# Weighing expert rows on ScalarE, moving layer 0's openings, and routing both choices at once in a two-layer kernel

## The chip, the cores and the metric

The kernel runs on one core of one Trainium2 chip. The metric is the device time of one execution in microseconds (us). The engines are named as in the profile: PE is TensorE (matmul), PEld its weight loads, DVE is VectorE, ACT is ScalarE, POOL is GpSimd, and SP is SyncE, which here only issues DMAs.

## What is computed

Two layers work on x of 2 x 2048 tokens by 256 channels. Each layer computes `x + s(xn) * silu(g(xn))`, where xn is the layer norm of x, s is one branch and g the other.

```
layer 0:  s = linear attention (16 heads of 16, rotary, elu + 1), times W_out
          g = block: h = ln(xn);  x' = xn + softmax attention(h) W_proj     (causal, per batch; 2048 tokens, 16 heads of 16)
              flat = ln(x');  gates = softmax(flat Wgate);  top 2 of 8 experts, 1024 slots for each expert
              exp_in[e, pos] = flat[token];  exp_out = gelu(exp_in W1 + b1) W2 + b2
              g = x' + sum over the 2 choices of gate * exp_out[e, pos]     (gate 0 where no slot is left)
layer 1:  s = softmax attention (causal; 16 heads, queries, keys and values of 32) Wo
          g = x int4(kernel) + bias + (x a) b
```

## The kernel before

Everything is float32 apart from small masks. Tokens stand in 32 tiles of 128 rows (`xr`, 16 tiles for each batch). The kernel has three stages: layer 0's attention with routing and linear attention; the experts; layer 1 with its attention and gate. Four heads share the 128 partitions, 32 rows for each, so that four score matmuls run side by side in row groups. A **head group** is four heads of one batch, and there are eight in each layer.

`run_attention` (L515) writes the attention of both layers in **units**. For a head group, pass A computes scores for the row maxima (tile t of queries against 512 keys, L536), which DVE reduces (L543 on the diagonal, L547 elsewhere). Pass B, started later, computes the transposed scores (L562), of which ACT takes the exponential (L574) into one of the tiles `pt`. A unit holds four matmuls of pass A and four pairs of pass B, and takes all 8 PSUM banks. Per group there are 40 units of pass A and 36 of pass B. After every second block of keys, and at the end of a block of 256 queries, follow the **sums** (L804 in layer 0; L1508 and L1514 in layer 1): column-tiled matmuls of `pt` with the values. In layer 1 POOL first adds up the exponentials (L1490 to L1495) for the denominators.

All other work is emitted as steps of **strands**: `prep` (norms and projections of the next head group, full-array matmuls), `lin` (linear attention, `lin_keys` and `lin_out`), `moe` (`route`), `send`, `end` (`finish`, `residual`), `mix`, `gate`. Every step names its engine, an expected cost, and what it reads and writes. The class `Plan` then orders all steps: a greedy beam search over the steps' costs, with a handicap for each strand, picks for each engine the next step that can start first. The resulting order of each engine is fixed in the program. Buffers (`Buf`) are taken from small sets of slots (8 banks `s`, and in layer 1 six `pt`, one `gx` and one `xs`), and a step that needs one waits until a slot is free.

PE work of strands other than `S` (full-array work) is let in only at an **opening**: before a unit whose first step has `open = True`, and up to 2.5 us of it (`LIMIT`); if nothing else can start for 0.3 us, it goes in anyway. Before the change, a unit is open if the unit before it was followed by sums or had no pass B:

```
            if first and (u == 0 or closed):
                first.open = True
            closed = late or not b
```

`route` (L898) works on four token tiles (two at the very end): it normalises them, computes the logits, and then DVE does some sixty small instructions on 128 x 32 or 128 x 4 elements: softmax and both choices (`choose`, L943), and after a matmul that counts tokens (`count`) the slots (`places`, L964). `places` loops over the two choices; for each it computes the slot for sending (`to`), the slot for fetching (`back`) and the weight (`m`). Then POOL issues one indirect DMA for each tile and choice (`send`, L991) into `slots_in`. The first load of the experts (L1284) waits for all sends.

The experts (L1274 to L1309) run as eight times two blocks of 512 rows, without a planner.

In layer 1, `mix` (L1343) finishes layer 0 for two token tiles: SP loads `xs` (the input and the linear attention's output), POOL issues four indirect gathers into `gx` (L1357), DVE weighs the rows of both choices and adds x' (L1366, L1367, L1370), ACT applies silu (L1373), and POOL multiplies by s and adds the input (L1374, L1375). After every second `mix` the moments (L477, DVE) and roots (L482 to L485, POOL) for the norm follow. The mixes of batch 0 come ahead of the first head group, those of batch 1 at units 24, 32, ... 80.

Of the kernel before, what the change touches and what calls it, by code (L numbers as in the profile page):

```python
# [317 lines left out]
def kernel(ctx: ExitStack, tc: tile.TileContext, i: dict, out: bass.AP):  # L318
# [34 lines left out]
    def turn_pair(pair, tp=None):  # L353
# [161 lines left out]
    def run_attention(plan, make, prepare, subtract, sum_keys, finish, last_sum, before=None, others=()):  # L515
# [65 lines left out]
        sums, parts_left, pair = {}, [], []  # L581
        for u in range(at + last_sum + 1):
# [60 lines left out]
    with ExitStack() as sc:  # L643
# [226 lines left out]
        SH = [P, 4, E]  # L870

        def small(name):
            return w.tile(SH, F32, name=name)

        def line(name):
            return w.tile([P, 4], F32, name=name)
# [4 lines left out]
        def expert_row(c, of):  # L881
            return cst[:, None, c : c + E].to_broadcast([P, of, E])
# [7 lines left out]
        def first_of_largest(m, hot, src, first):  # L890

            nc.vector.tensor_reduce(m, src, AX.X, ALU.max)
            nc.vector.tensor_tensor(hot, src, wide(m), ALU.is_equal)
            nc.vector.tensor_tensor(hot, hot, expert_row(C_EREV, src.shape[1]), ALU.mult)
            nc.vector.tensor_reduce(first, hot, AX.X, ALU.max)
            nc.vector.tensor_tensor(hot, hot, wide(first), ALU.is_equal)

        def route(G, t0, of):  # L898
            n0 = G.b * NT + t0
            gates, rest, mask, before_, took, *hots = (x[:, :of] for x in smalls)  # L900
            top, tot, first, place, e_of, room, a_ = (x[:, :of] for x in lines)
            ms = [m[:, n0 : n0 + of] for _, _, m in routes]
# [40 lines left out]
            def choose():  # L943
                nc.vector.tensor_reduce(tot, gates, AX.X, ALU.add)
                nc.vector.reciprocal(tot, tot)
                nc.vector.tensor_tensor(gates, gates, wide(tot), ALU.mult)
                first_of_largest(ms[0], hots[0], gates, first)
                nc.vector.scalar_tensor_tensor(rest, hots[0], -4.0, gates, ALU.mult, ALU.add)
                first_of_largest(ms[1], hots[1], rest, first)
                nc.vector.tensor_tensor(mask, hots[0], hots[1], ALU.add)  # L950
                nc.vector.tensor_copy(before_[:, 0:1], so_far)
                for n in range(1, of):
                    nc.vector.tensor_tensor(before_[:, n : n + 1], before_[:, n - 1 : n], mask[:, n - 1 : n], ALU.add)
                nc.vector.tensor_tensor(so_far, before_[:, of - 1 :], mask[:, of - 1 :], ALU.add)
# [5 lines left out]
            def count():  # L960
                for n, (ones_, m) in enumerate(((cst[:, C_TRI : C_TRI + P], mask), (ones, before_))):
                    nc.tensor.matmul(cum.t[:, : of * E], ones_, m.rearrange("p t e -> p (t e)"), start=n == 0, stop=n == 1)
# [21 lines left out]
            S("moe", "DVE", 3.2, choose, r=["gates"], w=["hots", "mask"])  # L984
            S("moe", "PE", 0.25, count, r=["mask"], w=[cum])
            S("moe", "DVE", 3.6, places, r=[cum, "hots"], w=[("routes", n0), "gates"])
            for t in range(of):
                for to, _, _ in routes:

                    def send(to=to, t=t):  # L990
                        inst = nc.gpsimd.indirect_dma_start(  # L991
                            out=slots_in, out_offset=bass.IndirectOffsetOnAxis(ap=to[:, n0 + t : n0 + t + 1], axis=0),
# [181 lines left out]
        for b in range(B):  # L1174
# [3 lines left out]
            start, every = ((4, 7.5), (180, 7.5))[b]  # L1178
# [8 lines left out]
        run_attention(plan, Group0, prepare, subtract, sum_keys, finish, SUM_LAG0, others=others)  # L1187
# [132 lines left out]
    with ExitStack() as sc:  # L1320
# [7 lines left out]
                mx=slots(wk, "mx", 2, [P, 2, 4, 4]), pt=slots(wk, "pt", 6, [P, 4, 512]), ps=slots(wk, "ps", 2, [P, 4, QC]),  # L1328
# [5 lines left out]
                gl=slots(wk, "gl", 2, [P, 2, D]), gs=slots(wk, "gs", 2, [P, 2, D]), gx=slots(wk, "gx", 1, [P, 2, 2, D]), xs=slots(wk, "xs", 1, [P, 2, 2, D]),  # L1334
# [8 lines left out]
        def mix(n0):  # L1343
# [20 lines left out]
            def weigh():  # L1364
                for t in range(2):
                    nc.vector.tensor_scalar_mul(gx.t[:, 0, t], gx.t[:, 0, t], routes[0][2][:, n0 + t : n0 + t + 1])  # L1366
                    nc.vector.scalar_tensor_tensor(  # L1367
                        gx.t[:, 0, t], gx.t[:, 1, t], routes[1][2][:, n0 + t : n0 + t + 1], gx.t[:, 0, t], ALU.mult, ALU.add
                    )
# [285 lines left out]
```

## Time and profile before

| | |
|---|---|
| median of three runs | 3568.2 us (3566.0 to 3568.63) |
| profiled execution | 3565.2 us, span 3563.4 us |
| granted PE clock, mean | 0.964 |
| layer 0's first sums to the last | 60.9 to 1453.0 us |
| head groups of layer 0, end to end of their sums | 165.0, 170.8, 194.2, 166.1, 159.6, 162.0, 178.2 us |
| experts | first transpose at 1507.5 us, last matmul to 1976.7 us |
| first matmul of layer 1 | 2012.4 us |
| head groups of layer 1, end to end of their sums | 208.1, 170.5, 194.7, 183.9, 168.1, 168.0, 149.5 us |

In the profile's slices a digit is the busy share of a fortieth of the span, 89.1 us, in tenths. Times of one place are in us from the start of the span. A group is all instructions of one line, engine and tile; "idle before" is the time its engine stood still just ahead of it, with what ended that. A head group's end is read from the last of its 576 matmul records of the sums' line.

### The profile page before, as it was taken

How to read it: one execution, taken by the hardware profiler on the slowest of the kernel's cores; microseconds unless marked ns; L12 is line 12 of the kernel's file. 1: busy time of each engine (PE TensorE's matmuls, PEld its weight loads, DVE VectorE, ACT ScalarE, POOL GpSimd, SP SyncE). 2: the span in 40 equal slices, each digit the busy share in tenths (PEclk: the TensorE clock that was granted, in tenths of full speed). 3: DMA queues.
4: the chain of work that ended last, by engine and by line, in shares of the span. 5: the costliest groups of instructions: out<-in, count | busy, mean ns of one | idle time of the engine just before them, and what ended most of it. 6: DMA issues, size and time to landing. Idle time of an engine off the chain costs nothing.

```text
span 3563.4 us, 81449 instructions
## 1 busy us (share of the span) xinstructions
PE 3381.1 (95%) x33814; PEld 2412.0 (68%) x33814; DVE 2193.3 (62%) x5726; ACT 1667.0 (47%) x3281; POOL 1679.8 (47%) x2238
## 2 busy tenths in 40 slices
PE   6999999999999999599999599989999999999998
PEld 4767777777777777366666356656777667777775
DVE  4767676777677768511111266777677557676774
ACT  3565555555555555221111154544455554544554
POOL 3452232333332221400000466887787567878777
PEclk7999999999999999799999789998999999999999
DMA  5000000000000000212220221111000010000000
GB/s 178 2 2 2 11 8 8 16 28 14 13 8 5 19 14 12 99 61 81 66 86 24 75 66 35 34 38 34 21 14 21 31 39 19 18 14 18 16 26 22
DMA packets 88020, 115.41 MB, mean 32 GB/s; under 512 B 9043, under 2 KB 67103, under 8 KB 87650
## 3 DMA queue, kind: packets, MB, share of 16 engines
q1 hardware_dynamic: 81506, 96.32, 8.3%
q0 software_dynamic: 6144, 13.88, 1.2%
q8 instruction: 266, 4.36, 0.5%
q14 instruction: 104, 0.85, 0.1%
HBM read 75.33 MB, written 37.75 MB: 32 GB/s over the span
## 4 chain that ended last, share of the span: by engine, by line
PE 84%; POOL 5%; DVE 5%; issue 3%; ACT 2%; DMA 1%; POOLq 0%; SPq 0%; DVEq 0%; ACTq 0%
PE s L562 16%; PE s L536 16%; PE s L804 7%; PE s L1297 6%; PE s L1303 6%; PE s L1508 6%; PE s L1420 3%; PE s L736 3%; PE s L506 3%; PE s L1478 2%; PE s L1514 2%; PE s L1556 2%; PE s L359 2%; PE s L1435 2%; PE s L1057 1%
## 5 line engine op out<-in xcount | busy, mean ns | idle before, releaser
L574 ACT ACTIVATE pt<-s 128x512 f32<-128x512 f32 (+1 forms) x2304 | 1170.2, 577 | 625.5 <-PE s L1478 192.2
L562 PE MATMUL s<-qt,kt 32*128 32x256 f32 (+1 forms) x9216 | 1329.0, 390 | 9.3 <-ACT pt L574 2.5
L536 PE MATMUL s<-kt,qt 32*128 32x512 f32 (+3 forms) x5120 | 1306.2, 563 | 21.1 <-DVE mx L547 11.4
L547 DVE TENSOR_REDUCE mx<-s 128x1 f32<-128x512 f32 x1536 | 958.6, 684 | 205.8 <-PE s L536 114.5
L562 PEld LDWEIGHTS s<-qt,kt 32*128 32x128 f32 x9216 | 1023.9, 186 | 66.9 <-ACT pt L574 13.2
L536 PEld LDWEIGHTS s<-kt,qt 32*128 32x128 f32 x5120 | 560.6, 187 | 170.0 <-issue 89.8
L543 DVE CUSTOM_DVE_ANT_0 s<-s,cst 128x128 f32<-128x128 f32 (+3 forms) x1024 | 480.8, 516 | 101.7 <-PE s L536 79.5
L1490 POOL TENSOR_TENSOR ps<-pt 128x1024 f32<-128x1024 f32 (+1 forms) x160 | 347.6, 2173 | 125.5 <-ACT pt L574 104.0
L743 POOL TENSOR_TENSOR ra<-raw,rope 128x128 f32<-128x128 f32 x128 | 59.3, 463 | 676.3 <-ACT raw L755 622.0
L1494 POOL TENSOR_TENSOR ps<-ps,pt 128x1024 f32<-128x1024 f32 x128 | 302.8, 2365 | 84.5 <-ACT pt L574 78.9
L1478 PE MATMUL s<-mh,ones_h 3*128 3x512 bf16 (+1 forms) x1152 | 316.9, 370 | 0.0
L1357 POOL DMA_INDIRECT gx<-slots_out,back x64 | 62.7, 980 | 499.0 <-issue 496.7
L1306 DVE TENSOR_TENSOR ye<-s,b 128x256 f32<-128x256 f32 x64 | 27.2, 425 | 410.7 <-PE s L1303 410.7
L804 PE MATMUL s<-pt,vt 128*32 128x256 f32 (+1 forms) x4608 | 272.6, 375 | 1.6 <-ACT pt L574 1.6
L1495 POOL TENSOR_TENSOR ps<-ps,pt 128x1024 f32<-128x1024 f32 (+1 forms) x128 | 268.1, 2095 | 10.0
L1508 PE MATMUL s<-pt,vt 128*32 128x256 f32 (+1 forms) x4608 | 271.7, 374 | 0.2 <-ACT pt L574 0.2
L1298 ACT ACTIVATE hm<-s,b1c 128x512 f32<-128x512 f32 x128 | 87.9, 687 | 361.1 <-PE s L1297 361.1
L1297 PE MATMUL s<-xt,w 128*128 128x512 f32 x512 | 226.1, 600 | 7.1 <-DVE xt L1269 7.0
L1508 PEld LDWEIGHTS s<-pt,vt 128*32 128x32 f32 x4608 | 134.5, 110 | 138.9 <-issue 20.7
L1303 PE MATMUL s<-w,hm 128*128 128x256 f32 x1024 | 223.6, 379 | 0.0
L804 PEld LDWEIGHTS s<-pt,vt 128*32 128x32 f32 x4608 | 134.5, 110 | 123.7 <-issue 25.0
L1303 PEld LDWEIGHTS s<-w,hm 128*128 128x128 f32 x1024 | 194.6, 190 | 33.3 <-issue 7.7
(256 smaller groups left out, 4289.7 us busy)
## 6 DMA issues: line engine op xcount, KB each, us to landing
w<-in_L_ffn_W_dram SPq DMA_DIRECT2D x16, 1024.0 KB, 5.6
gl<-g_dram SPq DMA_DIRECT2D x64, 256.0 KB, 2.6
slots_in<-zero SPq DMA_DIRECT2D x8, 1024.0 KB, 10.1
xe<-slots_in SPq DMA_DIRECT2D x16, 512.0 KB, 5.7
slots_out<-ye SPq DMA_DIRECT2D x16, 512.0 KB, 5.2
xr<-in_L_attn_x_dram SPq DMA_DIRECT2D x4, 1024.0 KB, 8.2
s_dram<-lo SPq DMA_DIRECT2D x16, 256.0 KB, 2.0
hn<-in_L_attn_x_dram SPq DMA_DIRECT2D x16, 256.0 KB, 2.7
```

What stands on the lines that cost most here:

```text
L536: nc.tensor.matmul(s.t[:, :w], g.qt.t[r, t * P : (t + 1) * P], g.kt.t[r, 512 * k : 512 * k + w], start=True, stop=True)
L543: nc.vector.tensor_tensor_reduce(s.t[:, :w], s.t[:, :w], causal[:, 512 - w :], 1.0, -3e38, ALU.add, ALU.max, to)
L547: nc.vector.tensor_reduce(to, s.t[:, :w], AX.X, ALU.max)
L562: nc.tensor.matmul(s.t[:, at], g.kt.t[r, kj * P : (kj + 1) * P], g.qt.t[r, QC * c + q0 : QC * (c + 1)], start=n == 0, stop=n == 1 and not ...
L574: S("B", "ACT", t_act(w), lambda: nc.scalar.activation(pt.t[:, j, :w], s.t[:, :w], AF.Exp, scale=0.25), r=[s], w=[(pt, j)])
L804: nc.tensor.matmul(av.t[32 * j : 32 * j + 32, q0:QC], vts[G.vn][:, kj, j], pt.t[:, j, at], start=n == 0, stop=n == len(tiles) - 1,)
L1297: nc.tensor.matmul(ps, w1[:, k, f * P : (f + 1) * P], xt[:, k], start=k == 0, stop=k == 1)
L1303: nc.tensor.matmul(ps[:, :D], hm[:, f, s * P : (s + 1) * P], w2[:, f], start=f == 0, stop=f == FF // P - 1)
L1478: return lambda: nc.tensor.matmul(s.t[:, :w_], ones_h[r], G.mh[c].t[r, 512 - w_ :], start=False, stop=last)
L1490: nc.gpsimd.tensor_tensor(ps.t[:, :, q0:], pt.t[:, :, same], pt.t[:, :, odd], ALU.add)
L1494: nc.gpsimd.tensor_tensor(ps.t, ps.t, pt.t[:, :, even], ALU.add)
L1508: nc.tensor.matmul(av.t[32 * j : 32 * j + 32, q0:QC], G.vt.t[:, kj, j], pt.t[:, j, at], start=n == 0, stop=False)
```

## The change

1. **Openings.** `run_attention` gets the argument `between`. In layer 0 (`between=True`) a unit is open if the unit before it was *not* followed by sums (or had no pass B). In layer 1 the rule is as before.
2. **Routing.** `to`, `back` and `m` of both choices lie in one tile each, and so do the intermediate values. The step `choose` is split into `largest` and `second`. `places` handles both choices in one instruction where it can, takes the expert's number from `first` rather than from a product and a sum, and ends with the slots for sending; the slots for fetching and the weights come in a step of their own, `ways_back`.
3. **Linear attention.** Batch 0's parts are emitted from unit 0 rather than 4.
4. **Mixes.** `gx` and `xs` have two slots each; `pt` has five instead of six. The two choices are weighed by ACT, one step for each, and DVE adds x' and the second choice in two steps. For batch 0 the product and the last sum are on DVE, for batch 1 on POOL.
5. **Costs.** Some costs that the planner reads are changed, in layer 1 those of POOL's sums from 2.2 and 4.4 us to 1.95 to 4.7.

```diff
-    routes = [
-        (rt.tile([P, NA], I32, name=f"to{n}"), rt.tile([P, NA], I32, name=f"back{n}"), rt.tile([P, NA], F32, name=f"m{n}"))
-        for n in range(2)
-    ]
+    to_, back_, m_ = (rt.tile([P, 2, NA], t, name=x) for x, t in (("to", I32), ("back", I32), ("m", F32)))
+    routes = [(to_[:, n], back_[:, n], m_[:, n]) for n in range(2)]
...
-    def run_attention(plan, make, prepare, subtract, sum_keys, finish, last_sum, before=None, others=()):
+    def run_attention(plan, make, prepare, subtract, sum_keys, finish, last_sum, before=None, others=(), between=False):
...
-            if first and (u == 0 or closed):
+            if first and opens:
                 first.open = True
-            closed = late or not b
+            opens = not b or (not late if between else late)
...
-        smalls = [small(x) for x in ("gates", "rest", "mask", "before", "took", "hot0", "hot1")]
-        lines = [line(x) for x in ("top", "tot", "first", "place", "e_of", "room", "a_")]
+        gates_, rest_, mask_, before_, took_ = (small(x) for x in ("gates", "rest", "mask", "before", "took"))
+        hots_ = small("hots", 2)
+        top_, tot_ = line("top"), line("tot")
+        first_, place_, e_of_, room_, a_ = (line(x, 2) for x in ("first", "place", "e_of", "room", "a_"))
...
-            def choose():
+            def largest():
                 nc.vector.tensor_reduce(tot, gates, AX.X, ALU.add)
                 nc.vector.reciprocal(tot, tot)
                 nc.vector.tensor_tensor(gates, gates, wide(tot), ALU.mult)
-                first_of_largest(ms[0], hots[0], gates, first)
-                nc.vector.scalar_tensor_tensor(rest, hots[0], -4.0, gates, ALU.mult, ALU.add)
-                first_of_largest(ms[1], hots[1], rest, first)
-                nc.vector.tensor_tensor(mask, hots[0], hots[1], ALU.add)
-                nc.vector.tensor_copy(before_[:, 0:1], so_far)
+                first_of_largest(m[:, 0], hots[:, 0], gates, first[:, 0])
+
+            def second():
+                nc.vector.scalar_tensor_tensor(rest, hots[:, 0], -4.0, gates, ALU.mult, ALU.add)
+                first_of_largest(m[:, 1], hots[:, 1], rest, first[:, 1])
+                nc.vector.tensor_tensor(mask, hots[:, 0], hots[:, 1], ALU.add)
...
             def places():
+
+
                 nc.vector.tensor_scalar_add(took, cum.t[:, : of * E].rearrange("p (t e) -> p t e", e=E), -1.0)
-                for n, (to, back, _) in enumerate(routes):
-                    nc.vector.tensor_tensor(gates, hots[n], took, ALU.mult)
-                    nc.vector.tensor_reduce(place, gates, AX.X, ALU.add)
-                    nc.vector.tensor_tensor(gates, hots[n], expert_row(C_EIDX, of), ALU.mult)
-                    nc.vector.tensor_reduce(e_of, gates, AX.X, ALU.add)
-
-                    nc.vector.tensor_scalar(a_, e_of, 4096.0, 4.0 * NSLOT, ALU.mult, ALU.add)
-                    nc.vector.tensor_scalar(room, place, float(CAP), None, ALU.is_ge)
-                    nc.vector.tensor_tensor(a_, a_, room, ALU.mult)
-                    nc.vector.scalar_tensor_tensor(a_, e_of, float(CAP), a_, ALU.mult, ALU.add)
-                    nc.vector.tensor_tensor(to[:, n0 : n0 + of], a_, place, ALU.add)
-                    nc.vector.tensor_scalar_min(a_, place, float(CAP - 1))
-                    nc.vector.scalar_tensor_tensor(back[:, n0 : n0 + of], e_of, float(CAP), a_, ALU.mult, ALU.add)
-                    nc.vector.tensor_scalar(room, place, float(CAP), None, ALU.is_lt)
-                    nc.vector.tensor_tensor(ms[n], ms[n], room, ALU.mult)
+                for n in range(2):
+                    nc.vector.tensor_tensor(hots[:, n], hots[:, n], took, ALU.mult)
+                nc.vector.tensor_reduce(place, hots, AX.X, ALU.add)
+                nc.vector.tensor_scalar(e_of, first, -1.0, float(E), ALU.mult, ALU.add)
+                nc.vector.tensor_scalar(a, e_of, 4096.0, 4.0 * NSLOT, ALU.mult, ALU.add)
+                nc.vector.tensor_scalar(room, place, float(CAP), None, ALU.is_ge)
+                nc.vector.tensor_tensor(a, a, room, ALU.mult)
+                nc.vector.scalar_tensor_tensor(a, e_of, float(CAP), a, ALU.mult, ALU.add)
+                nc.vector.tensor_tensor(to, a, place, ALU.add)
+
+            def ways_back():
+                nc.vector.tensor_scalar_min(a, place, float(CAP - 1))
+                nc.vector.scalar_tensor_tensor(back, e_of, float(CAP), a, ALU.mult, ALU.add)
+                nc.vector.tensor_scalar(room, place, float(CAP), None, ALU.is_lt)
+                nc.vector.tensor_tensor(m, m, room, ALU.mult)
             S("moe", "DVE", 0.35, less_top, r=[lg], w=["gates"])
             S("moe", "ACT", 0.25, lambda: nc.scalar.activation(gates, gates, AF.Exp), r=["gates"], w=["gates"])
-            S("moe", "DVE", 3.2, choose, r=["gates"], w=["hots", "mask"])
-            S("moe", "PE", 0.25, count, r=["mask"], w=[cum])
-            S("moe", "DVE", 3.6, places, r=[cum, "hots"], w=[("routes", n0), "gates"])
+            S("moe", "DVE", 1.7, largest, r=["gates"], w=["gates", "hot0"])
+            S("moe", "DVE", 2.4, second, r=["gates", "hot0"], w=["hots", "mask"])
+            S("moe", "PE", 0.5, count, r=["mask"], w=[cum])
+            S("moe", "DVE", 2.1, places, r=[cum, "hots"], w=[("routes", n0), "hot0", "hots", "places"])
+            S("moe", "DVE", 0.8, ways_back, r=["places"], w=["places"])
...
-            start, every = ((4, 7.5), (180, 7.5))[b]
+            start, every = ((0, 7.5), (180, 7.5))[b]
...
-        run_attention(plan, Group0, prepare, subtract, sum_keys, finish, SUM_LAG0, others=others)
+        run_attention(plan, Group0, prepare, subtract, sum_keys, finish, SUM_LAG0, others=others, between=True)
...
-                mx=slots(wk, "mx", 2, [P, 2, 4, 4]), pt=slots(wk, "pt", 6, [P, 4, 512]), ps=slots(wk, "ps", 2, [P, 4, QC]),
+                mx=slots(wk, "mx", 2, [P, 2, 4, 4]), pt=slots(wk, "pt", 5, [P, 4, 512]), ps=slots(wk, "ps", 2, [P, 4, QC]),
...
-                gl=slots(wk, "gl", 2, [P, 2, D]), gs=slots(wk, "gs", 2, [P, 2, D]), gx=slots(wk, "gx", 1, [P, 2, 2, D]), xs=slots(wk, "xs", 1, [P, 2, 2, D]),
+                gl=slots(wk, "gl", 2, [P, 2, D]), gs=slots(wk, "gs", 2, [P, 2, D]), gx=slots(wk, "gx", 2, [P, 2, 2, D]), xs=slots(wk, "xs", 2, [P, 2, 2, D]),
...
-            def weigh():
+            def weigh(n):
                 for t in range(2):
-                    nc.vector.tensor_scalar_mul(gx.t[:, 0, t], gx.t[:, 0, t], routes[0][2][:, n0 + t : n0 + t + 1])
-                    nc.vector.scalar_tensor_tensor(
-                        gx.t[:, 0, t], gx.t[:, 1, t], routes[1][2][:, n0 + t : n0 + t + 1], gx.t[:, 0, t], ALU.mult, ALU.add
-                    )
-                nc.vector.tensor_tensor(gx.t[:, 0], gx.t[:, 0], x, ALU.add)
-
-            S("mix", "DVE", 2.0, weigh, r=[(gx, n, t) for n in range(2) for t in range(2)] + xn, w=[gx])
+                    nc.scalar.mul(gx.t[:, n, t], gx.t[:, n, t], routes[n][2][:, n0 + t : n0 + t + 1])
+
+            got = [[(gx, n, 0), (gx, n, 1)] for n in range(2)]
+            for n in range(2):
+                S("mix", "ACT", 0.75, lambda n=n: weigh(n), r=got[n], w=got[n])
+            S("mix", "DVE", 1.0, lambda: nc.vector.tensor_tensor(gx.t[:, 0], gx.t[:, 0], x, ALU.add), r=[*got[0], *xn], w=got[0])
+            S("mix", "DVE", 1.0, lambda: nc.vector.tensor_tensor(gx.t[:, 0], gx.t[:, 0], gx.t[:, 1], ALU.add), r=[*got[0], *got[1]], w=[gx])
             S("mix", "ACT", 2.0, lambda: nc.scalar.activation(gx.t[:, 0], gx.t[:, 0], AF.Silu), r=[gx], w=[gx])
-            S("mix", "POOL", 1.26, lambda: nc.gpsimd.tensor_tensor(gx.t[:, 0], gx.t[:, 0], xs.t[:, 1], ALU.mult), r=[gx, xs], w=[gx])
-            S("mix", "POOL", 1.26, lambda: nc.gpsimd.tensor_tensor(x, gx.t[:, 0], xs.t[:, 0], ALU.add), r=[gx, xs], w=xn)
+
+            eng, cost, v = ("DVE", 0.7, nc.vector) if n0 < NT else ("POOL", 1.27, nc.gpsimd)
+            S("mix", eng, cost, lambda: v.tensor_tensor(gx.t[:, 0], gx.t[:, 0], xs.t[:, 1], ALU.mult), r=[gx, xs], w=[gx])
+            S("mix", eng, cost, lambda: v.tensor_tensor(x, gx.t[:, 0], xs.t[:, 0], ALU.add), r=[gx, xs], w=xn)
...
-            calls = [(1, lambda: S("pair", "POOL", 2.2 * len(pair), together, r=[(pt, j) for j in range(4)], w=[ps]))]
+            cost = (2.3 if not q0 else 1.95) if len(pair) == 1 else (4.7 if not q0 else 3.6)
+            calls = [(1, lambda: S("pair", "POOL", cost, together, r=[(pt, j) for j in range(4)], w=[ps]))]
```

More of the change, by code (lines that the diff above doesn't have):

```diff
@@ L580, in run_attention @@
             part()
-        sums, parts_left, pair = {}, [], []
+        sums, parts_left, pair, opens = {}, [], [], True
         for u in range(at + last_sum + 1):
@@ L867, in residual, with small, line @@
               r=[pr, ("xr", n0), ("xr", n0 + 1)], w=[("xr", n0), ("xr", n0 + 1)])
[L870 to L876, printed above, removed]
+        def small(name, *n):
+            return w.tile([P, *n, 4, E], F32, name=name)
+        def line(name, *n):
+            return w.tile([P, *n, 4], F32, name=name)
         def wide(a):
             return a[:, :, None].to_broadcast([P, a.shape[1], E])
-        def expert_row(c, of):
-            return cst[:, None, c : c + E].to_broadcast([P, of, E])
-        smalls = [small(x) for x in ("gates", "rest", "mask", "before", "took", "hot0", "hot1")]
-        lines = [line(x) for x in ("top", "tot", "first", "place", "e_of", "room", "a_")]
+        gates_, rest_, mask_, before_, took_ = (small(x) for x in ("gates", "rest", "mask", "before", "took"))
+        hots_ = small("hots", 2)
+        top_, tot_ = line("top"), line("tot")
+        first_, place_, e_of_, room_, a_ = (line(x, 2) for x in ("first", "place", "e_of", "room", "a_"))
         so_far = w.tile([P, 1, E], F32, name="so_far")
@@ L893, in first_of_largest @@
             nc.vector.tensor_tensor(hot, src, wide(m), ALU.is_equal)
-            nc.vector.tensor_tensor(hot, hot, expert_row(C_EREV, src.shape[1]), ALU.mult)
+            nc.vector.tensor_tensor(
+                hot, hot, cst[:, None, C_EREV : C_EREV + E].to_broadcast([P, src.shape[1], E]), ALU.mult
+            )
             nc.vector.tensor_reduce(first, hot, AX.X, ALU.max)
@@ L899, in route @@
             n0 = G.b * NT + t0
-            gates, rest, mask, before_, took, *hots = (x[:, :of] for x in smalls)
-            top, tot, first, place, e_of, room, a_ = (x[:, :of] for x in lines)
-            ms = [m[:, n0 : n0 + of] for _, _, m in routes]
+            gates, rest, mask, before, took = (x[:, :of] for x in (gates_, rest_, mask_, before_, took_))
+            top, tot, hots = top_[:, :of], tot_[:, :of], hots_[:, :, :of]
+            first, place, e_of, room, a = (x[:, :, :of] for x in (first_, place_, e_of_, room_, a_))
+            to, back, m = (x[:, :, n0 : n0 + of] for x in (to_, back_, m_))
             x2, lg = Buf("x2"), Buf("s")
@@ L952, in choose @@
+            def second():
+                nc.vector.scalar_tensor_tensor(rest, hots[:, 0], -4.0, gates, ALU.mult, ALU.add)
+                first_of_largest(m[:, 1], hots[:, 1], rest, first[:, 1])
+                nc.vector.tensor_tensor(mask, hots[:, 0], hots[:, 1], ALU.add)
+                nc.vector.tensor_copy(before[:, 0:1], so_far)
                 for n in range(1, of):
-                    nc.vector.tensor_tensor(before_[:, n : n + 1], before_[:, n - 1 : n], mask[:, n - 1 : n], ALU.add)
@@ L954, in choose @@
-                nc.vector.tensor_tensor(so_far, before_[:, of - 1 :], mask[:, of - 1 :], ALU.add)
+                    nc.vector.tensor_tensor(before[:, n : n + 1], before[:, n - 1 : n], mask[:, n - 1 : n], ALU.add)
+                nc.vector.tensor_tensor(so_far, before[:, of - 1 :], mask[:, of - 1 :], ALU.add)
             cum = Buf("s")
             def count():
-                for n, (ones_, m) in enumerate(((cst[:, C_TRI : C_TRI + P], mask), (ones, before_))):
-                    nc.tensor.matmul(cum.t[:, : of * E], ones_, m.rearrange("p t e -> p (t e)"), start=n == 0, stop=n == 1)
+                for n, (ones_, x) in enumerate(((cst[:, C_TRI : C_TRI + P], mask), (ones, before))):
+                    nc.tensor.matmul(cum.t[:, : of * E], ones_, x.rearrange("p t e -> p (t e)"), start=n == 0, stop=n == 1)
@@ L987, in route, with send @@
+            S("moe", "DVE", 2.1, places, r=[cum, "hots"], w=[("routes", n0), "hot0", "hots", "places"])
+            S("moe", "DVE", 0.8, ways_back, r=["places"], w=["places"])
             for t in range(of):
-                for to, _, _ in routes:
-                    def send(to=to, t=t):
+                for way, _, _ in routes:
+                    def send(way=way, t=t):
                         inst = nc.gpsimd.indirect_dma_start(
-                            out=slots_in, out_offset=bass.IndirectOffsetOnAxis(ap=to[:, n0 + t : n0 + t + 1], axis=0),
+                            out=slots_in, out_offset=bass.IndirectOffsetOnAxis(ap=way[:, n0 + t : n0 + t + 1], axis=0),
```

## The prediction

> **What bounds the kernel now.** I read the page's busy line and slices first, then the groups, then windows and the timeline at the places of the change.
>
> ```profile
> PE 3381.1 (95%) x33814; PEld 2412.0 (68%) x33814; DVE 2193.3 (62%) x5726; ACT 1667.0 (47%) x3281; POOL 1679.8 (47%) x2238
> ...
> PE   6999999999999999599999599989999999999998
> ...
> PEclk7999999999999999799999789998999999999999
> ```
>
> TensorE (PE) is covered in 95% of the span[...]. Two kinds of time are to be had: row-tiled scores that crawl inside busy stretches, and the visible holes in slices 17 (end of layer 0), 23 (start of layer 1) and 26 to 28.
>
> Layer 0's crawl shows in a window that holds exactly one unit of scores (4 tiles of pass A, 4 of pass B, 24 records) and two that hold a double unit with nothing between. Columns: window, length, busy PE, PEld, DVE, ACT, POOL, clock, DMA.
>
> ```profile
> 1003.77:1005.80 2.03, 2.03 (x25) 1.65 (x24) 0.87 (x2) 1.46 (x4) 1.47 (x2) 1.00 0.03 8
> 981.05:985.80 4.75, 4.75 (x52) 4.24 (x49) 4.75 (x14) 4.05 (x9) 1.74 (x2) 1.00 0.01 3
> 1029.19:1033.94 4.75, 4.75 (x52) 4.02 (x48) 4.02 (x7) 3.48 (x7) 0.00 (x0) 1.00 0.00 0
> ```
>
> A unit alone takes 2.03 us, two in a row 4.75: the second needs the 8 banks back, and VectorE (DVE) frees pass A's at 4 x 684 ns = 2.74 us a unit. If other PE work stands between, DVE drains behind it.
>
> Layer 1's holes:
>
> ```profile
> L1366 DVE TENSOR_SCALAR gx<-gx,m x16: 341/896/3018, 2171.1 to 2470.8; 128x256 f32<-128x256 f32 x16
> L1367 DVE SCALAR_TENSOR_TENSOR gx<-gx,m x16: 483/711/3147, 2171.8 to 2471.2; 128x256 f32<-128x256 f32 x16
> ...
> 2428.74 3.02 DVE L1366 TENSOR_SCALAR gx<-gx,m 128x256 f32<-128x256 f32 x1
> 2431.79 2.51 DVE L1367 SCALAR_TENSOR_TENSOR gx<-gx,m 128x256 f32<-128x256 f32 x1
> 2434.23 2.42 DVE L1366 TENSOR_SCALAR gx<-gx,m 128x256 f32<-128x256 f32 x1
> ...
> 2438.55 1.00 PE L536 MATMUL s<-kt,qt 32*128 32x384 f32 x1 [5.71 <-DVE mx L547]
> ...
> 2304.90:2513.00 208.10, 35.03 (x580) 17.11 (x576) 0.92 0.11 35
> 2513.00:2683.50 170.50, 33.55 (x580) 16.66 (x576) 1.00 0.05 16
> ```
>
> The weighing L1366/L1367 takes 0.35 and 0.48 us alone, up to 3 us beside POOL's sums. One weighing held DVE 9.1 us; the maxima (L547) behind it, and then PE, waited 5.71. The last two rows hold 576 L1508 records each, one head group: 208 us with five of batch 1's eight mixes in it, 170 without, at clock 0.92 against 1.00.
>
> [...]
>
> **The change, part by part.**
>
> (1) *Openings of layer 0.* Before, guests (full-array work) may go in ahead of a unit that follows sums, so PE ran unit, unit, sums, guests. Now they go in after a unit without sums: unit, guests, unit, sums. The written-out PE orders give the count: row blocks of one unit 123 to 229, of two 59 to 12, of three 13 to 11; all blocks 648 to 669, full-array blocks 241 to 205. From the trace (270 to 1380 us): one unit 2.10 us (2.32 after another single with under 2 us between), two 5.12. At 2.2 for a unit now: 47 x (5.12 - 4.4) = -34. Fewer full-array blocks: a fit of block time to content gives 0.26 us for each, 36 x 0.26 = -9, of which I take -5, since row blocks rise. Bounds: 0 if DVE becomes the pace anyway; 47 x (5.12 - 4.2) = -43, and -9. Lost cover: DVE is 66 of 89 us busy per slice here, so units of 3.5 us still fit its 2.74.
>
> (2) *Layer 0's end.* Guests get in later: the new order has two more output products of linear attention behind the last sums. They leave the busy stretch (two of some 7 us: -14). In the tail their chain (matmul 3.5 at half clock, POOL's rotation 4.2, exp, transposes) stands between the routes on PE, and its last rotation precedes the last four sends on POOL. Against it the routes shorten: after the shared first instruction, 13 for each choice become 9 for both until the slots are known, and 4 for the way back. At 0.2 us each the route before the last leaves DVE 2.7 us sooner; the last gains 0.6, as its second send came 1.85 us after its first instead of 1.27. By hand, from the last sums: 10 us to the product last but one, 21.5 for its chain, 4.7 for the last route's transposes and logits, 8 for choice, count and places, with POOL's rotation done at 45; four sends 5; then 13 to the first transpose of the experts, as now (1494.5 to 1507.5). That is 63 us instead of 53: +9 or 10. Net -5, bounds -14 to +10. The 117 route instructions taken off DVE elsewhere (23 us) lie beside PE: 0, covered by DVE's idle third. Linear attention starting four units earlier fills PE's idle opening with 3.4 us pieces: 0, bounds +-5.
>
> (3) *Start of layer 1.* One gather buffer makes eight mixes of 15 us each in series. With two, the POOL order is eight gathers, statistics, eight gathers. First pair: 8 x 1.25 (pitch of L1357), landing 2.7, weighing on ACT 2 x 0.51 (L717), two adds of 0.69 (L1370), silu 0.63 (L1373), product and sum on DVE instead of POOL 1.38 for 2.53, moments 1.0, roots 3.15, hand-overs 0.7: 21.3 us after 1981, against 30.7. So -9.5 for PE's first work. The later pairs come every 21.4 instead of 30.3; PE's holes between 2013 and 2170 sum to 10 us and the lowered clock costs up to as much; I take 8.5 of 20. Sum -18, bounds -5 to -28.
>
> (4) *Mixes of batch 1.* Off DVE: 2 x L1366, 2 x L1367, one L1370, about 7 us here (4.8 a mix over all sixteen by the groups' means, 2.4 to 2.8 for most of batch 0). On DVE: two adds, 0.69 to 2.72 each. ACT gets four of 0.51 us, two by two (32 us in all sixteen), exps queued behind; ACT is half idle. The holes between 2165 and 2480 sum to 27 us, lost clock (0.92 over 320 us, half of it felt) about 10; two thirds of 37 is -25, bounds -10 to -36. SP's loads of xs, one mix earlier now, stand ahead of the gates' loads there: 0, hidden by the 8 units between mixes.
>
> (5) *Paid for with one exp tile, six to five.* Sums come two units after the last of a pair, so five are live at most if POOL keeps up. It is the one added wait: an exp behind POOL's reading, with all exps behind it on ACT and PE's banks behind those. Before:
>
> ```profile
> ACT pt L574 <- POOL ps L1494: 13.0, 5, 2.9
> ```
>
> in 970 us with six. I take +4, bounds 0 to +20. New POOL costs reorder it: within that.
>
> Sum: -39 - 5 - 18 - 25 + 4 = **-83**. The profiled execution took 3565.2 us (span 3563.4 and 1.8 around it), 3.0 below the median 3568.2: 3482 by its clock, **3485** as a median.
>
> **Rivals.**
>
> *A: layer 0's openings bring nothing,* as DVE paces single units too: the 21 singles at 2.32 us point that way, the windows above against it. Of (1) and (2) only -7 of -44 is left: 3568 - 46 = 3522.
>
> *B: the mixes stay locked.* Two-input adds also wait for POOL (2.71 once in eight), and a weighing placed before its gather lands holds the exps. A third of (3) and (4), 14 of 43: 3568 - 54 = 3514.
>
> *C, slower: five exp tiles.* If each of 160 sums in layer 1 holds an exp behind POOL, which is 70 of 89 us busy, the wait decides from 87/160 = 0.54 us on (87 is the gain without the +4); at 0.65 us it gives 3568 + 104 - 87 = 3585. For: POOL ends many waits of the sums. Against: 15 us of such waits now, and the order of the changed layer 1 has hardly more double units together (three or more 10 to 17, two 70 to 62).
>
> *D: no change,* gains of DVE given back in a reordered plan: 3568.
>
> **How the numbers follow.** 0.2% (7 us) is about what a measurement of this kernel can tell from no change. As forecast 0.55 (3450 to 3510), A 0.17, B 0.13, C 0.09, D with small moves either way 0.06. Adding the bounds of (1) to (5) in quadrature gives about +-32; the range reaches down to 3445 and up past A and B to 3545. Faster: 0.55 + 0.17 + 0.13 + 0.03 = 0.88; same 0.03; slower 0.09.
>
> **What would show it.** Right: layer 0's head groups (576 L804 records each) fall from about 160 to 155 us; experts start within 10 us of 53 after the last sums; the first hn transpose comes 26 instead of 36 us after the last expert matmul; the second group of layer 1 falls from 208 to about 180; POOL-ended waits of exps stay under 30 us. Wrong: layer 0 groups as before (A), two-input adds of 2 us (B), or groups 3 to 8 of layer 1 above 170 us with exps waiting for POOL (C).

## The result, and the profile after

The changed kernel takes 3517.7 us (median of four runs, 3515.2 to 3523.5), the kernel before 3567.1 beside it: ratio 0.9864, 95% interval 0.9847 to 0.9881. That is 49 us where 83 were forecast. The profiled execution's span is 3517.3 us, 46.1 below the 3563.4 of before, and all stage times from here on are from such spans.

The page's busy line and slices, after:

```profile
PE 3354.9 (95%) x33814; PEld 2382.7 (68%) x33814; DVE 2160.5 (61%) x5577; ACT 1680.8 (48%) x3341; POOL 1653.3 (47%) x2222
...
PE   6999999999999999599999699999999999999998
...
PEclk7999999999999999699999899999999999999998
```

PE's share is 95% again, so it says nothing of the gain. The slices do: the hole at the start of layer 1 (slice 23) went from 5 to 6, slice 27 from 8 to 9, and the clock of slices 23, 24 and 28 from 7, 8, 8 to 8, 9, 9. Slice 17, the end of layer 0, is as hollow as before, at clock 6 instead of 7.

Where the 46.1 us came from, read from the matmul records (us):

| stretch | before | after | difference | forecast |
|---|---|---|---|---|
| start to last sums of layer 0 | 1453.0 | 1415.5 | -37.5 | -53 |
| last sums to the experts' first transpose | 54.4 | 76.3 | +21.9 | +9 |
| experts | 469.3 | 468.1 | -1.2 | 0 |
| last expert matmul to first hn transpose | 35.7 | 25.7 | -10.0 | -9.5 |
| to the end of layer 1's first head group | 292.5 | 274.0 | -18.5 | -8.5, and part of (4) |
| second group | 208.1 | 199.2 | -8.9 | the rest of -25 |
| groups 3 to 8 | 1034.7 | 1049.2 | +14.5 | +4 |
| end | 15.7 | 9.3 | -6.4 | 0 |

Two windows of layer 0 after, a single unit of scores and one of the double units that remain. Columns: window, length, busy PE, PEld, DVE, ACT, POOL, clock, DMA.

```profile
944.73:946.76 2.03, 2.03 (x27) 1.65 (x26) 1.12 (x2) 0.81 (x2) 0.00 (x0) 1.00 0.00 0
...
957.93:962.68 4.75, 4.75 (x54) 4.08 (x56) 4.15 (x14) 3.59 (x7) 1.53 (x6) 1.00 0.02 5
```

A unit is what it was, 2.03 alone and 4.75 for two. PE's records cover both windows from end to end, so the busy share does not show the crawl; the count does, 27 records in 2.03 us against 54 in 4.75. What changed is how many doubles (two complete units with nothing between) there are. Over all of layer 0 the records hold 50 doubles (mean 5.14 us) and 87 singles (2.10) before, 11 (5.22) and 189 (2.21) after. Counting each stretch of one kind of PE work up to the start of the next, row-tiled time (the scores) fell from 734.0 to 699.1 us and full-array time from 452.8 to 447.1 (240 blocks to 205), while column-tiled time (the sums) rose from 261.6 to 264.6. Of the 37.5 us, 11.9 fall in the first head group, which ends at 245.4 instead of 257.3.

The end of layer 0 after, from the timeline (start, duration, engine and line, in brackets the idle time before it and its releaser):

```profile
1457.29 0.59 PE L963 MATMUL s<-before,ones 128*128 128x16 f32 x2
...
1464.19 1.09 PE L1124 MATMUL s<-cst,lk 128*128 128x128 f32 x4 [6.31 <-DVE lk L1046]
1466.55 0.98 POOL L996 DMA_INDIRECT slots_in<-x,to  x1 [0.30 <-issue]
1470.83 3.78 PE L1156 MATMUL s<-wout,lf 128*128 128x256 f32 x8 [0.73 <-ACT lf L1159]
1475.26 0.34 SPq L1162 DMA_DIRECT2D s_dram<-lo  x1
1480.17 0.06 DVE L1254 MEMSET seven<- 128x1 f32 x1 [11.02 <-DMA s_dram<-lo]
1480.22 0.39 SPq L1281 DMA_DIRECT2D w<-in_L_ffn_W_dram  x1
...
```

The last send is issued at 1466.55, 51 us after the last sums, as worked out. But the experts' stage (its first instructions are the memset L1254 and the weights' loads L1281) starts at 1480, released by the store of linear attention's last output. Before, the sends ended the stage:

```profile
1493.56 0.98 POOL L991 DMA_INDIRECT slots_in<-x,to  x1 [0.30 <-issue]
1496.08 0.06 DVE L1249 MEMSET seven<- 128x1 f32 x1 [4.60 <-DMA slots_in<-x,to]
...
1507.41 1.30 PE L1291 MATMUL t<-cst,xe 128*128 128x128 f32 x5 [20.89 <-DMA xe<-slots_in]
```

From the end of the last send to the first transpose it was 13 us; after, with the transpose at 1491.7, it is 24.

Layer 1 after. First the window of the gaps in batch 1's mixes, before and after (columns as above), then PE's longest wait in it before and its waits after (total, times, longest):

```profile
2160.00:2480.00 320.00, 292.16 (x3075) 201.23 (x3071) 229.69 (x483) 153.16 (x273) 257.72 (x236) 0.92 0.13 39
```

```profile
2130.00:2440.00 310.00, 292.20 (x3276) 201.28 (x3271) 217.50 (x497) 172.12 (x321) 275.75 (x258) 0.98 0.13 41
```

```profile
PE s L536 <- DVE mx L547: 9.5, 2, 5.7
```

```profile
PE s L1522 <- POOL ps L1502: 5.8, 5, 1.6
PE s L1471 <- POOL mpad L1467: 3.4, 3, 1.6
PE s L1522 <- POOL ps L1499: 3.4, 3, 1.4
...
PE s L535 <- DVE mx L546: 0.4, 1, 0.4
```

PE stands idle 17.8 us of the window after, 27.8 before, at clock 0.98 instead of 0.92. Waits on DVE's maxima fell from 9.5 us to 0.4. What ends PE's waits now is POOL: its sums before the denominators' matmuls (L1522) 9.2 us, the maxima's rows (`mpad`) 3.4.

### The profile page after: what moved, and what is told of

Read it like the earlier page. It is cut to its first block, busy times and chain, and to the rows that moved or that the text cites. A ratio compares the mean times of both kernels' runs of the same rounds, so it can differ in the third digit from the quotient of the medians.

```text
span 3517.3 us, 81236 instructions
## 1 busy us (share of the span) xinstructions
PE 3354.9 (95%) x33814; PEld 2382.7 (68%) x33814; DVE 2160.5 (61%) x5577; ACT 1680.8 (48%) x3341; POOL 1653.3 (47%) x2222
## 4 chain that ended last, share of the span: by engine, by line
PE 80%; POOL 11%; DVE 3%; issue 2%; ACT 2%; DMA 1%; SPq 0%; POOLq 0%; ACTq 0%; DVEq 0%
PE s L561 15%; PE s L535 14%; PE s L803 7%; PE s L1302 6%; PE s L1308 6%; PE s L1516 5%; PE s L1427 3%; PE s L504 3%; PE s L735 3%; POOL ps L1501 2%; PE s L1485 2%; POOL ps L1502 2%; POOL ps L1497 2%; PE s L359 2%; PE s L1522 2%
## 5 line engine op out<-in xcount | busy, mean ns | idle before, releaser
L561 PE MATMUL s<-qt,kt 32*128 32x256 f32 (+1 forms) x9216 | 1297.6, 391 | 7.5 <-DVE un L810 3.3
L535 PE MATMUL s<-kt,qt 32*128 32x512 f32 (+3 forms) x5120 | 1269.8, 561 | 5.1 <-ACT pt L573 2.0
L561 PEld LDWEIGHTS s<-qt,kt 32*128 32x128 f32 x9216 | 990.2, 187 | 61.3 <-ACT pt L573 9.8
L535 PEld LDWEIGHTS s<-kt,qt 32*128 32x128 f32 x5120 | 531.5, 187 | 165.0 <-issue 97.0
L1497 POOL TENSOR_TENSOR ps<-pt 128x1024 f32<-128x1024 f32 (+1 forms) x160 | 343.2, 2145 | 150.0 <-ACT pt L573 129.2
L1501 POOL TENSOR_TENSOR ps<-ps,pt 128x1024 f32<-128x1024 f32 x128 | 302.4, 2363 | 68.4 <-ACT pt L573 63.8
L1502 POOL TENSOR_TENSOR ps<-ps,pt 128x1024 f32<-128x1024 f32 (+1 forms) x128 | 269.9, 2109 | 10.0
L803 PEld LDWEIGHTS s<-pt,vt 128*32 128x32 f32 x4608 | 135.3, 111 | 125.3 <-issue 21.9
## 6 DMA issues: line engine op xcount, KB each, us to landing
slots_in<-zero SPq DMA_DIRECT2D x8, 1024.0 KB, 10.1
```

Of the source, the lines that this page charges most:

```text
L535: nc.tensor.matmul(s.t[:, :w], g.qt.t[r, t * P : (t + 1) * P], g.kt.t[r, 512 * k : 512 * k + w], start=True, stop=True)
L561: nc.tensor.matmul(s.t[:, at], g.kt.t[r, kj * P : (kj + 1) * P], g.qt.t[r, QC * c + q0 : QC * (c + 1)], start=n == 0, stop=n == 1 and not ...
L803: nc.tensor.matmul(av.t[32 * j : 32 * j + 32, q0:QC], vts[G.vn][:, kj, j], pt.t[:, j, at], start=n == 0, stop=n == len(tiles) - 1,)
L1497: nc.gpsimd.tensor_tensor(ps.t[:, :, q0:], pt.t[:, :, same], pt.t[:, :, odd], ALU.add)
L1501: nc.gpsimd.tensor_tensor(ps.t, ps.t, pt.t[:, :, even], ALU.add)
```

## The experiments

Twelve kernels ran in three series: `e1` to `e4`, `e5` to `e8` on another chip, and `e9` to `e12` on the first chip again. The kernel before took 3567.6, 3588.2 and 3566.1 us in them, so totals are compared within a series, by the ratio to before. The changed kernel without edits, run again in the third series, gave 0.9872 (0.9844 to 0.9899). Stage times come from one profiled execution each. "The theory" and "the rival" below say which part of the expectation quoted just before came out.

### Openings alone, and all but the openings

`e1_openings_only`: the kernel before with

```diff
-            closed = late or not b
+            opens = not b or (not late if between else late)
...
-SUM_LAG0, others=others)
+SUM_LAG0, others=others, between=True)
```

> The kernel before with nothing changed but layer 0's openings. Theory (openings cause all of layer 0's change, for good and ill): the last sums of layer 0 end near 1416 us instead of 1453, and the experts start about 76 us after them instead of 54, so the total is 3567 - 37 + 22 = 3552. Rival (the routes and the earlier linear attention give part of it): sums end at 1430 or later, total above 3558. Second rival (the longer tail comes from the routes' new steps, not from the openings): tail near 54 us, total near 3530.

`e2_no_openings`: the changed kernel with the old rule (`between=True` left out).

> The changed kernel with layer 0's openings as they were before. Theory: layer 0 is back at 1453 us for its last sums and 54 us (2 or 3 less by the shorter routes) from there to the experts, so the total is the changed kernel's 3518 plus 13 to 16: 3531 to 3534. Rival (routes and earlier linear attention matter by themselves): the experts start by 1495, total 3518 to 3525.

Measured: openings alone 3544.4 us, ratio 0.9939 (0.9923 to 0.9956); all but the openings 3520.3, 0.9872 (0.9856 to 0.9889). Added to the kernel before, the new rule brings the last sums 39.2 us earlier: row-tiled time falls by 22.7 and full-array time by 15.1. So the mechanism holds and rival A falls, and the first experiment's theory came out, with a shorter end (69.1 us instead of 76). In the second the rival came out. On top of the other parts the rule brings the last sums 24.7 us earlier (rows give 20.1, full-array work 9.1, and column-tiled work takes 4.6 more), but nothing that can be told at the experts' start: they start at 1488.9 us without it, and at 1491.7 and 1484.3 in two profiles with it. What eats the gain is the stretch behind the last sums. It grows from 54.4 to 69.1 with the openings alone, where the sends end 56.2 us after the last sums instead of 41.5, and from 48.8 to 76.3 on top of the rest.

### Where the end of layer 0 went

`e4_lin_earlier`: the changed kernel with batch 1's linear attention let in from unit 150 instead of 180.

```diff
-            start, every = ((0, 7.5), (180, 7.5))[b]
+            start, every = ((0, 7.5), (150, 8.0))[b]
```

> The changed kernel with the parts of batch 1's linear attention emitted from unit 150 every 8 units instead of from 180 every 7.5. Theory (the tail of layer 0 grew because linear attention's last products stood in it): the time from the last sums to the experts falls from 76 to about 55 us, the last sums end 0 to 14 us later since the work moves back among the units, total 3498 to 3512. Rival (the tail is the routes' own chain, or the planner leaves other work behind): tail stays above 70, total 3515 to 3522.

Measured: 3506.2 us, ratio 0.9827 (0.981 to 0.9843), the lowest time and ratio of all versions, and better than the changed kernel: the theory. The stretch behind the last sums falls from 76.3 to 55.2 us. The last sums come 3 us later than in the changed kernel's first profile and 11 later than in its second. (The profiled execution, 3515.4 us, is the longest of the four.) From its timeline:

```profile
1459.93 0.97 POOL L996 DMA_INDIRECT slots_in<-x,to  x1 [0.30 <-issue]
...
1462.46 0.06 DVE L1254 MEMSET seven<- 128x1 f32 x1 [6.43 <-DMA slots_in<-x,to]
...
1473.94 1.30 PE L1296 MATMUL t<-cst,xe 128*128 128x128 f32 x5 [20.26 <-DMA xe<-slots_in]
```

The memset is released by the sends again and the transpose comes 13 us after the last of them. So the late store of linear attention cost the changed kernel some 11 us there. All five profiles with the changed kernel's order in layer 0 (`after`, `e5`, `e6`, `e7`, `e11`) have the store as releaser and 24 us; all the others have the sends and 13. The other 10 are the sends, which end 42 us after the last sums here and 52 in the changed kernel, where the chain stands between the routes. At the experts' start this version is 33.5 us ahead of before; the changed kernel was 15.7, and 23.1 in its second profile.

### The routes alone

`e9_routes_only`: the kernel before with the routing of both choices in one, and nothing else.

> The kernel before with the routing of the changed one, nothing else. Theory (the routes' fewer DVE instructions gave most of the 13 us at the last sums and 5 us in the tail that the changed kernel without its openings had): last sums at 1440 to 1446 us, 49 to 52 us from there to the experts, ratio to before 0.995 to 0.997. Rival (linear attention's earlier start, or another order, gave it; 117 instructions of 0.2 us lie beside PE, as the prediction had it): last sums within 4 us of 1453, 51 to 54 us to the experts, ratio 0.998 to 1.000.

Measured: 3551.8 us, ratio 0.9956 (0.9942 to 0.997); the last sums come 11.4 us earlier and the stretch behind them shrinks by 1.9, to 52.5 us: the theory, with a stretch 0.5 longer. Groups 2 and 3 are as before to 0.1 us; group 4, with three routes in it, gives 9.7. Its window, before and with the routes alone:

```profile
593.00:787.20 194.20, 189.80 (x1945) 140.57 (x1942) 151.16 (x489) 103.71 (x217) 58.97 (x141) 0.96 0.06 19
```

```profile
593.10:777.60 184.50, 183.51 (x1940) 138.68 (x1936) 144.50 (x450) 102.64 (x215) 55.91 (x130) 0.97 0.06 20
```

DVE is busy 151 of 194 us there, 78%, against the 61 or 62% of the whole span. With 39 instructions and 6.7 us less on DVE the group is 9.7 us shorter, so here DVE had no idle third to hide them in. The records show where the time went. Before, three doubles of the group held 7, 11 and 20 route instructions on DVE, and took 23.9 us instead of the 15 of three plain ones:

```profile
652.60:659.82 7.22, 6.72 (x68) 5.12 (x64) 6.81 (x25) 3.33 (x7) 0.57 (x3) 1.00 0.01 2
720.30:729.26 8.96, 7.61 (x53) 6.00 (x55) 7.56 (x25) 3.89 (x7) 6.05 (x7) 0.81 0.25 90
766.70:774.38 7.68, 6.64 (x52) 4.88 (x48) 7.16 (x33) 3.96 (x7) 4.84 (x5) 0.91 0.19 68
```

With the routes alone no double beside routes takes more than 5.6 us. The number of doubles hardly changed (50 before, 51 here), yet row-tiled time fell by 10.8. Each of the other three kernels with the old routing (`e1`, `e3`, `e10`) has two or more such doubles of 8.2 to 9.6 us. A draw can move the last sums as much (below), and whether fewer instructions or their new places did it is not parted.

### The planner's draw

The planner breaks ties with a seeded draw, and any edit changes its order. To see how much of a difference is the draw's:

`e8_other_draw`: the changed kernel, `random.Random(0)` to `random.Random(1)`.

> The changed kernel with the planner's random draws started from 1 instead of 0, so that each layer has another order of the same quality by the planner's own measure. This sizes what an order alone is worth. Theory (orders matter little): last sums of layer 0 within 8 us of 1415, every group of layer 1 within 5 us, total 3510 to 3526. Rival (differences of 10 to 25 us between the variants of layer 0 are the draw's): last sums or the tail move by more than 10 us, total outside that.

`e10_before_other_draw`: the same in the kernel before.

> The kernel before with the planner's draws started from 1. Theory (an order alone is worth 10 us and more, so the edits of layer 0 can't be told apart finer than that): last sums, tail or a group of layer 1 move by 8 us or more, ratio to before 0.993 to 1.006. Rival (the order of before is typical): every stage within 5 us, ratio 0.998 to 1.002.

`e11_after_again`: the changed kernel, unedited, in the third series.

> The changed kernel once more, unedited, as the measure of what differs between chips. Theory: stages repeat within 2 us where the chip is like the first, ratio 0.985 to 0.988; on a chip where the kernel before takes about 3588 us, layer 0's last sums come at 1425 to 1432 and layer 1's first group takes 290 us instead of 274, at the same ratio.

`e12_lin_earlier_draw`: the edit of `e4_lin_earlier` with `random.Random(2)`.

> The changed kernel with batch 1's linear attention from unit 150 every 8 units, and the planner's draws from 2: an order in which no product of linear attention stands behind the last sums and only 6 row blocks have three units. Theory: last sums 1405 to 1420 us, 48 to 55 us to the experts, ratio to before 0.979 to 0.983, so faster than the changed kernel. Rival (its gain in layer 0 is lost to a worse draw in layer 1): ratio 0.984 to 0.988.

Measured: `e8_other_draw` 0.9832 (0.9816 to 0.9849), with 51.2 us behind the last sums instead of the 76 of the other kernels of its series (the rival); `e10_before_other_draw` 1.0037 (1.0022 to 1.0051), its last sums 21 us later and the stretch behind them 9 shorter (the theory; its profile is the second longest of nine executions, 7.6 us above the median); `e12_lin_earlier_draw` 3509.2 us, 0.9841 (0.9819 to 0.9864), with 55.4 (the rival: no better than `e4_lin_earlier`). In `e11_after_again` the ratio came as expected and the stages did not: the last sums came at 1408.0 us, 7.5 earlier than in the first profile, of which groups 5 and 8 hold 4.5 and 3.9; the stretch behind them, 76.3, and layer 1's first two groups are the same to 0.5. So one draw moves layer 0 by 10 to 20 us and a repeat by 7, and parts of layer 0 can't be told apart more finely than that. It doesn't make the whole change: every version of the changed kernel is 1.0 to 1.7% ahead. In the written-out orders `e8_other_draw` has one linear-attention output behind the last sums, as the kernel before, the changed kernel three, and the two kernels with linear attention earlier none.

### Buffers, DVE and POOL in layer 1

`e7_one_buffer`: the changed kernel with `gx` and `xs` one slot each and six `pt` again.

> The changed kernel with one gx, one xs and six exp tiles as before, weighing still on ACT. Theory (the second buffer gives the earlier start of layer 1, the weighing on ACT the rest): the first transpose of layer 1 comes 33 to 36 us after the last expert instead of 25.7, the time from there to the end of the first group stays within 10 us of 274, the second group stays near 199 us; total 3522 to 3535. Rival (the earlier start comes from ACT's weighing and from product and sum on DVE): transpose at 26 to 29 us, total 3515 to 3521.

`e5_dve_product`: product and last sum of batch 1's mixes on DVE too.

```diff
-            eng, cost, v = ("DVE", 0.7, nc.vector) if n0 < NT else ("POOL", 1.27, nc.gpsimd)
+            eng, cost, v = ("DVE", 0.7, nc.vector)
```

> The changed kernel with the product and the last sum of batch 1's mixes on DVE too, instead of on POOL. Theory (in the second group of layer 1 POOL, 89% busy, has become the pace; sums on PE wait for its ps): POOL loses 2.5 us a mix, the group falls from 199 us to 190 or less, total 3505 to 3512. Rival (DVE's two-input instructions, 1.6 to 2.7 us beside POOL, are the pace): DVE gets 1.4 to 5 us more a mix, the group goes to 205 or more, total 3520 to 3535.

`e6_pool_adds`: the two adds of batch 1's mixes on POOL instead of DVE.

> The changed kernel with the two adds of batch 1's mixes on POOL instead of DVE. Theory (POOL is the pace of layer 1's second group): 2.5 us more POOL a mix, the group goes from 199 to 205 or more, total 3522 to 3535. Rival (DVE held by two-input adds is the pace): DVE gets 1.6 + 1.8 us a mix back, the group falls to 190 or less, total 3505 to 3512.

Measured: `e7_one_buffer` 0.99 (0.988 to 0.992); the first hn transpose comes 31.7 us after the last expert matmul, 25.6 to 26.3 with two slots in the other kernels of the series, so the second slot makes 6 of the 10 us and the cheaper chain of each mix the rest: between theory and rival. `e5_dve_product` 0.9884 (0.9868 to 0.9901) and `e6_pool_adds` 0.9898 (0.9877 to 0.9919): the second group takes 196.5 and 192.8 us, groups 2 to 4 together 560.6 and 574.1, against 199.2 and 560.5 in the changed kernel, which did not run on this chip (`e8_other_draw`, with another order, has 197.7 there). Less on POOL doesn't shorten the stretch as it should if POOL set its pace, and less on DVE doesn't as it should if DVE's long adds did. Neither of the figures expected for the group, 190 or less or 205 or more, came in either run. Both are inconclusive: moves of this size are within what another order does.

What the mixes' operations cost beside POOL, from the tile `gx` after (times min/median/max in ns, first and last start):

```profile
L1371 ACT ACTIVATE gx<-gx,m x32: 494/509/530, 2142.1 to 2415.2; 128x256 f32<-128x256 f32 x32
...
L1376 DVE TENSOR_TENSOR gx<-gx,xr x8: 927/1572/2698, 2145.6 to 2420.9; 128x512 f32<-128x512 f32 x8
L1377 DVE TENSOR_TENSOR gx<-gx x8: 680/1758/2746, 2150.5 to 2422.5; 128x512 f32<-128x512 f32 x8
```

The weighing on ACT takes 0.49 to 0.53 us, and no longer inside a sum of POOL's (0.51 at 2145.1 and 2380.4, within L1497). ACT's table loads, 1.28 us each, are 36 after and 40 before, none of them at L1371. The adds on DVE take 0.68 or 0.69 us with POOL idle, 1.6 to 1.8 at the median here: half of rival B is true. Still, a mix of batch 1 holds DVE for 3.3 us on average, where its five instructions held it for 6.4 before.

### One exp tile fewer

`e3_five_exp_tiles`: the kernel before with `pt` five instead of six.

> The kernel before with five exp tiles in layer 1 instead of six, alone. Theory (five tiles cost what layer 1's later groups lost in the changed kernel): 4 to 8 us more, 3571 to 3575, layer 0 unchanged. Rival (tiles are free, the 8 us of the later groups come from another order): 3565 to 3569. Rival of the prediction (each sum holds an exp): 3640 or more.

Measured: 3564.6 us, ratio 0.9994 (0.9985 to 1.0002). It costs nothing: the rival that tiles are free. Of ACT's waits, those for POOL's reading rose from 15.2 us to 20.8 (2500 to 3470 us), without a cost in the total. The largest, with five tiles in the kernel before, and then two in the changed kernel, from 2440 to 3430 us (groups 3 to 8):

```profile
ACT pt L574 <- POOL ps L1494: 18.3, 7, 3.3
```

```profile
ACT pt L573 <- POOL ps L1501: 6.7, 3, 3.2
...
ACT pt L573 <- POOL ps L1497: 2.5, 1, 2.5
```

In the changed order exps wait 10.1 us in all for POOL's reading, less than before with six tiles: rival C falls.

## Why the prediction was right or wrong

The direction holds, and so does the outer range of 3445 to 3545 us. The inner range, 3450 to 3510 for "as forecast", does not: 3517.7 lies between the figures of rival B (3514) and rival A (3522), so the total alone could not have told them apart. The sum was too large by 37 us, 28 of them in layer 0 and 10 in layer 1.

**(1) Openings: mechanism right, size helped by luck, and not additive.** Doubles do crawl and singles do not: 5.14 us against 2.21 after, where 5.12 and 2.2 were used. The blocks came as counted (647 and 669 in the records, 648 and 669 in the orders), but the 47 doubles include some with an incomplete unit; complete ones fell by 39. Rows gave 34.8 us in all, as if to the forecast of 34. But the openings alone give 22.7 (`e1_openings_only`), and the routes alone give 10.8 in rows (`e9_routes_only`), for which the forecast had nothing. Of layer 0's gain 11.9 us lie in the first head group: the openings alone bring 3.8 there, all but the openings nothing. The earlier start of batch 0's linear attention, put at 0, was not run alone, so this stays open.

**(2) Layer 0's end: the step that failed.** The two late output products came as written, and the sends ended at 52 us where 50 were worked out. The failed sentence is "then 13 to the first transpose of the experts, as now": it held the last send to be the last thing the experts wait for. The transpose came 24 us after the last send, because the store of the last linear-attention output, issued at 1475.3 and landed at 1480.0, released the experts' stage; +9 became +22. `e4_lin_earlier` shows it by taking that chain away. Why a stage that reads none of that output waits for it is not shown; the code ends layer 0's buffers there, so reuse of their memory is the author's guess.

Two more terms failed. "0, covered by DVE's idle third" for the route instructions: `e9_routes_only` shows about 14 us, most of it in the group where DVE is 78% busy. Here the error was in the other direction. And the -14 for work that leaves the busy stretch is not to be seen: with the 5 of (1), full-array time should have fallen by 19, and it fell by 5.7 (6.0 in `e11_after_again`). Draws differ by as much, so why stays open.

**(3) Start of layer 1: right.** -10.0 against -9.5 for the first transpose. (The terms listed add up to 22.0 us rather than 21.3, which makes it -8.7.) The 8.5 for the pairs behind it can't be parted from (4): the first group's end came another 18.5 us earlier.

**(4) Mixes of batch 1: right in kind, smaller in the second group.** The wait named, DVE's maxima behind the weighing, fell from 9.5 to 0.4 us, and the clock came back from 0.92 to 0.98. (The lost clock in that sum, 0.08 x 320 us and half of it felt by the author's estimate, is 12.8 rather than about 10.) The group fell to 199, not 180; with the first group, (3) and (4) give 37.4 of 43. New ends took over a part: POOL's sums and rows, 12.6 us of PE's waits. In the kernel before, L1366, L1367 and L1370 took 0.34 to 0.36, 0.48 to 0.49 and 0.69 us with POOL idle, over all sixteen mixes. Each that took at least 0.1 us longer than that, up to 3.02, 3.15 and 2.72, overlaps one of POOL's sums (L1490 to L1495). The two adds after (L1376, L1377) took 0.68 to 0.69 us with POOL idle, and those above 0.7, up to 2.75, again all overlap a sum (L1497 to L1502), which takes 2.2 to 2.4 on average there (L1497, L1501, L1502). So a mix has two DVE instructions that grew beside the sums instead of five. Why they grow was not shown. That this gave the gain is read from the waits: no run puts the weighing back on DVE by itself. In the second group, 30 us above the third's 169, PE stands idle for 13 us and has a clock of 0.50 for 10, an estimated 5 us more by these figures. What causes this and the rest stays open, since neither `e5_dve_product` nor `e6_pool_adds` moved it clearly.

**(5) Five exp tiles: +4 forecast, 0 shown** by `e3_five_exp_tiles`. Groups 3 to 8 and the end took 8 us more after, and nothing here puts that down to the tiles. The order of the changed layer 1 differs, and no run parts its causes.

**Rivals.** A is refuted by `e1_openings_only`, C by `e3_five_exp_tiles`, D by the result. B is half right: the adds do wait, yet the mixes gained.

Of the signs named, layer 0's groups fell as said where no route stands (groups 2, 6 and 7: 165.0, 159.6 and 162.0 us to 162.6, 155.6 and 152.6; group 3 by 11.9, while of those with routes groups 5 and 8 fell by 1.1 and 2.9 and group 4 rose from 194.2 to 200.0). The hn transpose came at 26 us, and POOL-ended waits of exps stayed small. The experts' start within 10 us of 53 and the second group at about 180 did not come.

## What to carry to other kernels

When work is let in later, find the last consumer of everything that is moved, also of what is only stored: here a stage that reads nothing of a store waited for it. A mean busy share hides nothing locally; before costing removed instructions at nothing, read the engine's share in the stretch where they stand. With a planner that orders all, cost parts together, and run another draw before believing a difference of 10 us.

## What the runs showed of the hardware

- The same order repeats closely in some places and not in others. Groups 2 and 3 of `e9_routes_only` are within 0.1 us of the kernel before, in another series. On the chip of the second series the kernel before took 3588.2 us instead of 3566 to 3568. There the changed kernel's order of layer 0 (`e5` to `e7`) has groups 2, 3, 6 and 7 within 0.3 us of the first chip's, but 210 to 213 us for group 4 instead of 200, and layer 1's first group takes 289 to 294 us instead of 274 (there the edits and orders differ as well).
- Idle PE went with a lower clock. Around batch 1's mixes PE was idle for 27.8 of 320 us before, and the trace's record of the granted clock has 48 us at 0.50, in seven stretches of 3.4 to 10.2 us; after, it was 17.8 us of 310, and one stretch of 10.2. Six of the seven stretches before follow 5 us with 1.25 to 3.8 us of idle PE. The seventh and the one after follow only 0.2 and 0.1 us, so idle time as the records have it is not all of it. At the start of layer 1 before, PE was busy 5.7 of the 40 us from 1980 at a clock of 0.52. In layer 0's tail the output product of linear attention took 3.58 us at 0.53 before (L1151, at 1459.1) and 3.78 at 0.50 after. How much of the lost clock reached the end was not measured.
- Score matmuls of different row groups overlap. In the single unit after, the first four of both passes start within 0.03 us (944.67 to 944.70), and a record takes 0.4 to 0.7 us.
